# A four-layer graph network on one core: layer 0's results loaded by quarters, row stores on ScalarE, the last half block finished tile by tile

## The chip, the cores and the metric

The kernel runs on one core of a Trainium2 chip. The metric is the device time of one execution in microseconds. A core has TensorE (PE in the profile, with its weight loads as PEld), VectorE (DVE), ScalarE (ACT), GpSimd (POOL) and SyncE (SP), which work side by side and wait for each other by semaphores, and 16 DMA engines that move data between the main memory and the on-chip memory. A DMA is issued by an engine's instruction stream: SP, ACT or POOL. If an instruction there has to wait, those behind it wait too.

## What is computed

Four layers run one after the other over x (16 batches, 1024 nodes, 256 features) with one sparse matrix adj (1024 x 1024). Everything is float32.

```python
# layer 0
S   = sigmoid(relu(h_u @ W1[:d] + h_v @ W1[d:] + b1) @ W2 + b2)      # one score for each pair u, v
a_t = einsum('buv,bud->bvd', S * adj, h)
m_t = einsum('uv,bud->bvd', adj, h) * h
z   = beta1 * h + beta2 * (a_t @ Wa + ba) + beta3 * (m_t @ Wm + bm)
# layer 1
z   = z + relu((adj @ z) @ W.T + b)
# layers 2 and 3 (each)
feats = data @ W1.T
f1    = feats @ W2 + b2
coefs = softmax(leaky_relu(f1[:, :, None] + f1[:, None, :]) + adj, axis=-1)
out   = coefs @ feats + bias2 + data
```

## The kernel before

Because adj is sparse, the scores S are made only for its non-zeros. An earlier part of the program lists them for each node (up to 32 slots, the first 16 of each node and the rest packed into extra rows). There is a second arm of the program (from L1435 on) for a dense adj; it doesn't run here.

The 16 batches are worked in NGR = 4 groups of GB = 4.

*The scores*, `score_steps` (L717), are a generator of small steps: POOL gathers rows of v_d (L708), DVE adds and takes the relu and the weights (L825, L827), ACT sums (L831), and POOL scatters finished scores to a dense table in main memory, `dense_d` (L713). They are not a stage of their own: `Side.along` (L888) lets each step of the main work pay for a fraction of such a step (`PACE`), so that they run beside the matmuls, a group ahead of where they are used.

*The main work of a group.* `score_free` (L942) has earlier made the part of layer 0 that needs no scores and stored it by batch in `zb_d`, features on the partitions, 1024 nodes twice (for the two halves of the features), 1 MB a batch. For each group there follow:

- `with_edges` (L1120), the stage the first part of the change touches. It goes over four blocks of QN = 256 columns (v = 0 to 3), and in each block over eight tiles ut of 128 source nodes. Below, a *unit* is one (v, ut). In a unit, SP loads a piece of the score table, `gd` (512 KB, four buffers, `load_gd`, L904), ACT copies it to `gc` in another order (L1129, two buffers), and PE multiplies: 4 batches x 2 feature halves = 8 products, 16 matmul instructions of 256 columns. At the end of a block DVE adds the eight sums to the block's columns of z (L1152). The batches' z tiles must have been loaded from zb_d by then. In group 0, SP also loads the turned adj (`adj_sb<-adjT_d`, 512 KB each, eight of them) in odd units of the blocks 1 and 2, and ACT takes its exponential (L1118) in the blocks 2 and 3.
- `layer_one` (L1202): `projected` (L1157) makes the rows y, `neighbours` (L1185) multiplies them with pieces `adjT_in` (three buffers) that SP loads at L1191.
- `front` and `sums` (L1004, L1085) for layers 2 and 3. `sums` sums two half blocks of nodes (v = 0, 1), four tiles of 128 nodes each, and ends with `finish`: that of layer 2 is in `second` (L1267), that of layer 3 in `third` (L1297).

*The z loads.* `load_z` (L916) takes four z tiles and appends their loads to the list `z_loads`. For groups 1 to 3, `group_layers` (L1355) of the group before takes three of them from the list near its end (`next_z`, L1367); what remains is done in `with_edges` (L1136): one load of a whole 1 MB tile in every even unit, until the list is empty. For group 0 all four are loaded there, in the units 0, 2, 4 and 6 of block 0. For the later groups only the fourth is, in unit 0.

*What orders the work.* `paced` (L123) makes an instruction wait until PE has finished the product that was recorded some number of products back: 12 for a z load, 24 for a gd load, 16 for an adj_sb load and for a gc copy. The rest of the order on each engine comes from the order of the program, in which the framework may move loads ahead; on SP all loads and stores of this part stand in one stream.

*The last group* treats its batches in two pairs. While the first pair does layer 1, the second pair's rows y are made by `far_ahead` (L1401) and stored to `y_d` (L1404, eight stores of 256 KB). `by_lists` (L1207) gathers such rows with POOL along the lists and sums them on DVE (L1244), for the first six node tiles, with some sums stored to `part_d` by SP (L1248); all of this runs beside PE's work on the first pair.

*Layer 3's end*, `third`'s `finish` (L1318), handles two tiles at a time: two ACT copies out of the sums, one reciprocal on DVE of the two weights' totals, two DVE steps that divide and add the residual (L1328), and one store of 256 KB. Stores are put in the list `later`, and issued by ACT a tick later (L1333, shown in the profile at the caller's lines L998 and L1002).

Of the kernel before, what the change touches and what calls it, by code (L numbers as in the profile page):

```python
# [11 lines left out]
F32 = mybir.dt.float32  # L12
I32 = mybir.dt.int32
U32 = mybir.dt.uint32
AF = mybir.ActivationFunctionType
ALU = mybir.AluOpType
AX = mybir.AxisListType
P = 128

GB = 4  # L20
# [50 lines left out]
def gnn_stack_kernel(  # L71
# [27 lines left out]
    nc = tc.nc  # L99
    B, N, D = x.shape  # L100
# [3 lines left out]
    NV = N // HN  # L104
    HT = HN // P
    QN = HN // 2
# [3 lines left out]
    small = ctx.enter_context(tc.tile_pool(name="small", bufs=4))  # L110
    psum = []

    def bank():
        return psum[-1].tile([P, HN], F32, tag="bank", name="bank")
# [8 lines left out]
    def paced(ins, back=6):  # L123


        if recent:
            after(tc, ins, [recent[max(0, len(recent) - back)]], mybir.DependencyClass.Sync, "keeps pace")
        return ins
# [122 lines left out]
    zb_d = dram.tile([B, P, DH * N], F32, name="zb_d")  # L251
# [41 lines left out]
    def node_pairs(t):  # L293
        return t.rearrange("p (h n) -> p h n", h=DH)
# [80 lines left out]
    with ExitStack() as stack:  # L375
# [15 lines left out]
        for t in range(NT):  # L391
# [10 lines left out]
            out=below, in_=ones, pattern=[[1, P]], compare_op=ALU.is_gt, fill=0.0, base=0, channel_multiplier=-1,  # L402
# [40 lines left out]
        for t in range(NT):  # L443
# [5 lines left out]
            for r in range(SLOTS // 8):  # L449
                s = slice(8 * r, 8 * r + 8)  # L450
                nc.vector.max(out=slot_a[:, t, s], in_=src)
                if r < SLOTS // 8 - 1:
                    nc.vector.match_replace(
                        out=left, in_to_replace=slot_a[:, t, s], in_values=src, imm_value=-1.0
# [12 lines left out]
        ps = bank()  # L467
# [36 lines left out]
        to = prep1.tile([P, NF], F32, name="to")  # L504
# [183 lines left out]
    with tc.If(listed > 0) as arm:  # L688
        with ExitStack() as stack:
# [226 lines left out]
            def load_z(g):  # L916

                z = [node_pairs(wide_z.tile([P, DH * N], F32, tag="wide", name="z")) for _ in range(GB)]

                def load(i):  # L920
                    return nc.sync.dma_start(z[i], node_pairs(zb_d[g * GB + i]))

                z_loads.extend((load, i) for i in range(GB))
                return z

            z_loads = []
# [56 lines left out]
            four = stack.enter_context(tc.tile_pool(name="four", bufs=4, reuse_waits="tile"))  # L983
# [7 lines left out]
            later = []  # L991
# [128 lines left out]
            def with_edges(g, hw, z):  # L1120

                doing[0] = "edges"
                for v in range(N // QN):
                    cols = slice(v * QN, (v + 1) * QN)
                    acc = [[bank() for _ in range(DH)] for _ in range(GB)]
                    for ut in range(NT):
                        gd = first_gd.pop(0) if first_gd else load_gd(g, v, ut, back=BACK)
                        gc = gc_pool.tile([P, GB, QN], F32, tag="gc", name="gc")
                        paced(nc.scalar.activation(gc, gd.rearrange("p n i -> p i n"), AF.Copy), 16)  # L1129
                        for i in range(GB):  # L1130
                            for eh in range(DH):
                                product(
                                    acc[i][eh][:, :QN], hw[i][:, ut, eh * P : (eh + 1) * P], gc[:, i, :],
                                    start=ut == 0, stop=ut == NT - 1,
                                )
                        if z_loads and ut % 2 == 0:  # L1136
                            load, i = z_loads.pop(0)
                            paced(load(i), 12)
                        if (to_load or to_exp) and ut % 2 and v:
                            if v > 1 and to_exp:  # L1140
                                exponential(to_exp.pop(0))
                            if to_load:
                                jt = to_load.pop(0)
                                paced(nc.sync.dma_start(ea[:, jt, :], adjT_d[jt]), 16)
                                to_exp.append(jt)
                        yield 3.4 if g or v else 1
                    if v == N // QN - 1:
                        while to_exp:
                            exponential(to_exp.pop(0))
                    for i in range(GB):  # L1150
                        for eh in range(DH):
                            nc.vector.scalar_tensor_tensor(  # L1152
                                z[i][:, eh, cols], acc[i][eh][:, :QN], zbias[:, eh : eh + 1], z[i][:, eh, cols],
                                ALU.add, ALU.add,
                            )

            def projected(z, keep=None):  # L1157

                doing[0] = "one"
                y = [node_major("y") for _ in range(2)]  # L1160
                for jt in range(0, NT, 2):
                    for i in range(2):
                        ps = bank()
                        for k in range(2):
                            for dh in range(DH):
                                product(
                                    ps[:, k * D : (k + 1) * D], z[i][:, dh, (jt + k) * P : (jt + k + 1) * P],
                                    l1wT[:, dh, :], start=dh == 0, stop=dh == DH - 1,
                                )
                        nc.scalar.activation(  # L1170
                            y[i][:, jt : jt + 2, :], ps.rearrange("p (t d) -> p t d", t=2), AF.Copy
                        )
                        if keep:
                            keep(i, slice(jt, jt + 2), y[i][:, jt : jt + 2, :])
                        yield 1.7
                return y
# [120 lines left out]
            def third(z, i, b):  # L1297
                turned_back = []

                def early(v, jt):  # L1300
                    if v == 0 and jt == 2:
                        for dh in range(DH):
                            nc.scalar.activation(
                                z[i][:, dh, :], z[i][:, dh, :], AF.Identity, bias=gat3.bias2[:, dh : dh + 1]
                            )
                    if jt < NT - 2:
                        return
                    ps = bank()
                    for k in range(2):
                        it = v * HT + (jt - NT + 2) * 2 + k  # L1310
                        for dh in range(DH):
                            nc.tensor.transpose(
                                ps[:, k * D + dh * P : k * D + (dh + 1) * P],
                                z[i][:, dh, it * P : (it + 1) * P], ident,
                            )
                    turned_back.append(ps)

                def finish(v, acc):  # L1318
                    for c in range(0, HT, 2):
                        ps = turned_back.pop(0)  # L1320
                        it = v * HT + c
                        st = four.tile([P, 2, D + 1], F32, tag="st", name="st")
                        share = small.tile([P, 2], F32, tag="share", name="share")
                        for k in range(2):
                            nc.scalar.activation(st[:, k, :], acc[c + k][:, : D + 1], AF.Copy)  # L1325
                        nc.vector.reciprocal(share, st[:, :, D])
                        for k in range(2):
                            nc.vector.scalar_tensor_tensor(  # L1328
                                st[:, k, :D], st[:, k, :D], share[:, k : k + 1], ps[:, k * D : (k + 1) * D],
                                ALU.mult, ALU.add,  # L1330
                            )
                        to = out[b + i, it * P : (it + 2) * P].rearrange("(t p) d -> p t d", p=P)
                        later.append([1, functools.partial(nc.scalar.dma_start, to, st[:, :, :D])])  # L1333
                return finish, early

            def pair_layers(b, z, first):
# [64 lines left out]
            def far_ahead(z, main):  # L1401

                both = y_d.rearrange("(t p) (i d) -> p t i d", p=P, i=2)
                y = yield from projected(z, lambda i, ts, y: nc.sync.dma_start(both[:, ts, i, :], y))  # L1404
                gone, far = 0.0, Side(by_lists(msg))
                rest = neighbours(y, z, slice(FAR * P, N))

                def slots():
                    nonlocal gone
                    for us in itertools.chain(rest, main):  # L1410
                        gone += us
                        yield us * (0.68 if gone < 82 else 0.61)

                far.along(slots(), dict.fromkeys(PACE, 1))
                for _ in far.steps:
                    pass
                yield 0

            msg = []
            for g in range(NGR):  # L1420
                hw, z = loaded.pop(0)
# [141 lines left out]
```

## Time and profile before

| | |
|---|---|
| three runs, median | 3143.56 us (3133.77 to 3150.67) |
| profiled execution | 3123.2 us |
| its span, first to last instruction | 3121.5 us |
| mean granted clock of TensorE | 0.998 |
| PE busy | 3074.8 us (99% of the span) |
| DVE, ACT, POOL busy | 2352.6, 1945.1, 1878.9 us |
| moved by DMA | 700 MB, 224 GB/s on average |
| edge stage of group 0, first to last matmul | 942.07 to 1062.74 us |
| edge stages of groups 1, 2, 3 begin at | 1495.49, 2045.31, 2598.04 us |

In the profile's lists a row has the start in us, the length in us, the engine, the line of the kernel, the operation, what it writes `<-` what it reads, and how many such instructions were merged into the row (x64). A float32 product is two matmul instructions. What stands in square brackets is idle time of that engine just before the row, and whose result ended it. SPq and ACTq are DMA issues by SP and ACT, with the time that the issue took, not the transfer. A table by stretches has for each stretch the busy time of the five engines, the granted clock, the mean busy share of the 16 DMA engines and what they moved in GB/s.

### The profile page before, as it was taken

What the parts mean: (1) busy time and instruction counts of PE and PEld (TensorE: products, weight loads), DVE (VectorE), ACT (ScalarE), POOL (GpSimd) and SP (SyncE); (2) the same over time, 40 slices, a digit from 0 to 9 for tenths busy, and PEclk for the clock granted to TensorE, in tenths of its full rate; (3) what the DMA queues carried; (4) which work ended last, traced back from release to release, by engine and by line L of the source; (5) the groups of instructions that cost most, each with busy time, mean ns of one, the idle gap of its engine ahead of it and who ended that gap; (6) DMA issues with size and microseconds to landing.
All of it is one profiled execution on the core that took longest, in us unless ns stands there. A gap on an engine that the chain in (4) does not pass through costs nothing. (4 is left out here: it accounts for less than half of the span.)

```text
span 3121.5 us, 39024 instructions
## 1 busy us (share of the span) xinstructions
PE 3074.8 (99%) x11954; PEld 2179.2 (70%) x11954; DVE 2352.6 (75%) x3183; ACT 1945.1 (62%) x6520; POOL 1878.9 (60%) x1483
## 2 busy tenths in 40 slices
PE   9999999999999999999999999999999999999999
PEld 5544555545547756888875688888568888858888
DVE  7887777768774678999667899966789982157844
ACT  3345565656667876787887677788667764414242
POOL 1156787777664577777666776766777770076600
PEclk9999999999999999999999999999999999999999
DMA  9998898888889776568877665887765565485500
GB/s 321 331 331 310 270 313 260 273 242 253 254 290 331 229 214 202 156 185 285 285 233 207 209 165 171 266 284 232 219 206 164 159 207 166 132 262 156 164 2 28
DMA packets 288420, 699.96 MB, mean 224 GB/s; under 512 B 46141, under 2 KB 141178, under 8 KB 281034
## 3 DMA queue, kind: packets, MB, share of 16 engines
q0 software_dynamic: 128224, 387.80, 42.5%
q1 hardware_dynamic: 132538, 258.46, 23.7%
q10 hardware_dynamic: 27440, 51.13, 4.3%
q8 instruction: 96, 1.57, 0.2%
q14 instruction: 122, 1.00, 0.1%
HBM read 565.83 MB, written 131.41 MB: 223 GB/s over the span
## 5 line engine op out<-in xcount | busy, mean ns | idle before, releaser
L831 ACT ACTIVATE z<-z 128x256 f32<-128x256 f32 x2432 | 979.0, 406 | 574.1 <-DVE z L827 549.0
L825 DVE TENSOR_TENSOR z<-z,u 128x1024 f32<-128x1024 f32 x608 | 738.9, 1220 | 374.8 <-PE bank L131 262.4
L131 PE MATMUL bank<-feats,m 128*128 128x257 f32 x4096 | 909.0, 380 | 0.7 <-ACT st L1325 0.5
L708 POOL DMA_INDIRECT z<-v_d,slot_v x512 | 662.2, 1293 | 376.0 <-ACT z L831 208.1
L131 PEld LDWEIGHTS bank<-feats,m 128*128 128x128 f32 x4096 | 769.4, 190 | 111.2 <-ACT st L1325 1.3
L713 POOL DMA_INDIRECT dense_d<-gt,slot_at x512 | 674.5, 1317 | 184.4 <-issue 130.3
L827 DVE SCALAR_TENSOR_TENSOR z<-z,w2r 128x1024 f32<-128x1024 f32 x608 | 737.3, 1219 | 9.0
L131 PE MATMUL bank<-gc,hw 128*128 128x256 f32 x2048 | 451.8, 382 | 15.6 <-ACT gc L1129 10.5
L831 ACT ACTIVATION_READ_ACCUMULATOR z<-z 128x1 f32 x2432 | 461.6, 190 | 0.0
L131 PE MATMUL bank<-adj_sb,h 128*128 128x512 f32 x1024 | 442.3, 592 | 3.3 <-ACT st L333 2.0
L131 PEld LDWEIGHTS bank<-gc,hw 128*128 128x128 f32 x2048 | 386.6, 190 | 80.2 <-ACT gc L1129 20.7
L1099 DVE SCALAR_TENSOR_TENSOR m<-rho,tau,adj_sb 128x512 f32<-128x512 f32 x512 | 375.8, 742 | 65.6 <-PE bank L131 62.7
L131 PE MATMUL bank<-adjT_in,y 128*128 128x512 f32 (+1 forms) x960 | 403.4, 581 | 6.0 <-DMA adjT_in<-adjT_d 5.9
L131 PEld LDWEIGHTS bank<-adj_sb,h 128*128 128x128 f32 x1024 | 194.3, 190 | 242.7 <-issue 237.5
L131 PEld LDWEIGHTS bank<-adjT_in,y 128*128 128x128 f32 x960 | 182.0, 191 | 221.0 <-issue 203.8
L131 PE MATMUL bank<-w,hT 128*128 128x512 f32 (+1 forms) x1024 | 334.9, 487 | 0.0
L1129 ACT ACTIVATE gc<-gd 128x1024 f32<-128x1024 f32 x128 | 264.7, 2069 | 88.4 <-PE bank L131 74.9
L131 PEld LDWEIGHTS bank<-w,hT 128*128 128x128 f32 x1024 | 194.8, 191 | 141.5 <-issue 118.4
L131 PE MATMUL bank<-g_wT,z 128*128 128x257 f32 x1024 | 231.4, 380 | 1.6 <-ACT st L1325 1.1
L131 PEld LDWEIGHTS bank<-g_wT,z 128*128 128x128 f32 x1024 | 191.8, 190 | 33.2 <-issue 3.1
L708 POOL DMA_INDIRECT z<-v_d,x_node x96 | 124.2, 1294 | 128.6 <-ACT z L831 96.6
L1152 DVE SCALAR_TENSOR_TENSOR z<-bank,zbias,z 128x256 f32<-128x256 f32 x128 | 54.6, 480 | 111.7 <-PE bank L131 111.4
(168 smaller groups left out, 2379.4 us busy)
## 6 DMA issues: line engine op xcount, KB each, us to landing
gd<-dense_d SPq DMA_DIRECT2D x128, 512.0 KB
dense_d<-zero ACTq DMA_DIRECT2D x64, 512.0 KB
adjT_in<-adjT_d SPq DMA_DIRECT2D x112, 256.0 KB
h<-in_x_dram SPq DMA_DIRECT2D x19, 1024.0 KB
u_d<-st SPq DMA_DIRECT2D x64, 256.0 KB
v_d<-st SPq DMA_DIRECT2D x64, 256.0 KB
hw_d<-st SPq DMA_DIRECT2D x64, 256.0 KB
u<-u_d POOLq DMA_DIRECT2D x32, 512.0 KB
```

Source lines behind the costliest of these rows:

```text
L131: recent.append(nc.tensor.matmul(*args, **kw))
L708: return nc.gpsimd.indirect_dma_start(out=dst, out_offset=None, in_=src[:], in_offset=bass.IndirectOffsetOnAxis(ap=at, axis=0), **how,)
L713: return nc.gpsimd.indirect_dma_start(out=dst[:], out_offset=bass.IndirectOffsetOnAxis(ap=at, axis=0), in_=src, in_offset=None,)
L825: paced(nc.vector.tensor_tensor(z, z, u, ALU.add))
L827: nc.vector.scalar_tensor_tensor(zk, zk, 0.0, w2r[:, None, :].to_broadcast([P, GB, D]), ALU.max, ALU.mult)
L831: nc.scalar.activation(zk[:, c, :], zk[:, c, :], AF.Copy, accum_out=s[:, k, c : c + 1])
L1099: nc.vector.scalar_tensor_tensor(m, r[:, cols], ta[:, kt : kt + 1], ea[:, kt, cols], ALU.max, ALU.mult)
L1129: paced(nc.scalar.activation(gc, gd.rearrange("p n i -> p i n"), AF.Copy), 16)
L1152: nc.vector.scalar_tensor_tensor(z[i][:, eh, cols], acc[i][eh][:, :QN], zbias[:, eh : eh + 1], z[i][:, eh, cols], ALU.add, ALU.add,)
```

## The change

There are three edits.

1. A z load can load one quarter of a tile: the 256 columns of block v, for both feature halves, 256 KB. `with_edges` no longer empties `z_loads` in block 0. It keeps the list over the four blocks and loads, in even units, the quarter of each tile that belongs to the block at hand; the list is cleared after the last block. Group 0 so has sixteen loads of 256 KB, four in each block, in place of four of 1 MB in block 0. Groups 1 to 3 load the quarters of their fourth tile in unit 0 of each block. The three tiles that `next_z` loads are loaded whole as before.
2. The eight stores of `far_ahead` to `y_d` are issued by ACT, not SP.
3. In the last half block of the last batch, `finish` handles one tile at a time: four rounds of one copy, one reciprocal, one dividing step and one store of 128 KB, where there were two rounds of double size; and these four stores are issued by SP, not ACT. All other half blocks stay as they were.

```diff
-                def load(i):
-                    return nc.sync.dma_start(z[i], node_pairs(zb_d[g * GB + i]))
+                def load(i, v=None):
+                    cols = slice(None) if v is None else slice(v * QN, (v + 1) * QN)
+                    return nc.sync.dma_start(z[i][:, :, cols], node_pairs(zb_d[g * GB + i])[:, :, cols])
...
-                        if z_loads and ut % 2 == 0:
-                            load, i = z_loads.pop(0)
-                            paced(load(i), 12)
+                        if ut % 2 == 0 and ut // 2 < len(z_loads):
+                            load, i = z_loads[ut // 2]
+                            paced(load(i, v), 12)
...
                     if v == N // QN - 1:
+                        z_loads.clear()
                         while to_exp:
...
                 def finish(v, acc):
+                    last = b + i == B - 1 and v == NV - 1
                     for c in range(0, HT, 2):
                         ps = turned_back.pop(0)
                         it = v * HT + c
-                        st = four.tile([P, 2, D + 1], F32, tag="st", name="st")
-                        share = small.tile([P, 2], F32, tag="share", name="share")
-                        for k in range(2):
-                            nc.scalar.activation(st[:, k, :], acc[c + k][:, : D + 1], AF.Copy)
-                        nc.vector.reciprocal(share, st[:, :, D])
-                        for k in range(2):
-                            nc.vector.scalar_tensor_tensor(
-                                st[:, k, :D], st[:, k, :D], share[:, k : k + 1], ps[:, k * D : (k + 1) * D],
-                                ALU.mult, ALU.add,
-                            )
-                        to = out[b + i, it * P : (it + 2) * P].rearrange("(t p) d -> p t d", p=P)
-                        later.append([1, functools.partial(nc.scalar.dma_start, to, st[:, :, :D])])
+
+                        for ks in ((0,), (1,)) if last else ((0, 1),):
+                            n, k0 = len(ks), ks[0]
+                            st = four.tile([P, 2, D + 1], F32, tag="st", name="st")[:, :n, :]
+                            share = small.tile([P, 2], F32, tag="share", name="share")[:, :n]
+                            for k in ks:
+                                nc.scalar.activation(st[:, k - k0, :], acc[c + k][:, : D + 1], AF.Copy)
+                            nc.vector.reciprocal(share, st[:, :, D])
+                            for k in ks:
+                                nc.vector.scalar_tensor_tensor(
+                                    st[:, k - k0, :D], st[:, k - k0, :D], share[:, k - k0 : k - k0 + 1],
+                                    ps[:, k * D : (k + 1) * D], ALU.mult, ALU.add,
+                                )
+                            to = out[b + i, (it + k0) * P : (it + k0 + n) * P].rearrange("(t p) d -> p t d", p=P)
+                            queue = nc.sync if last else nc.scalar
+                            later.append([1, functools.partial(queue.dma_start, to, st[:, :, :D])])
...
-                y = yield from projected(z, lambda i, ts, y: nc.sync.dma_start(both[:, ts, i, :], y))
+                y = yield from projected(z, lambda i, ts, y: nc.scalar.dma_start(both[:, ts, i, :], y))
```

## Prediction

> **What bounds the kernel now.** I read the page's busy times first, then the busy times by stretch with the DMA share, then the PE timeline of the stage that adds layer 0's edge part, then what SP and ACT did there, and last the row stage and the tail.
>
> ```profile
> PE 3074.8 (99%) x11954; PEld 2179.2 (70%) x11954; DVE 2352.6 (75%) x3183; ACT 1945.1 (62%) x6520; POOL 1878.9 (60%) x1483
> ```
>
> TensorE is busy 99% of 3121.5 us, so only what removes a hole in PE's stream (46.7 us in all) or shortens the tail can help. A group's edge stage has four blocks of columns (v = 0 to 3), each of 128 matmul instructions of 256 columns. At group 3, where nothing disturbs it, 512 of them take 2598.04 to 2708.55, 110.5 us, or 0.216 each. At group 0 they take 942.07 to 1062.74, 120.7 us: about 10 us of holes. By blocks v = 0 to 3 of group 0 (columns: us, then busy of PE, PEld, DVE, ACT, POOL, then clock, DMA share, GB/s):
>
> ```profile
> 942.07:973.65 31.58, 27.97 (x129) 23.98 (x128) 8.31 (x14) 19.34 (x32) 11.71 (x11) 1.00 0.99 362
> 973.65:1002.60 28.95, 28.16 (x129) 23.82 (x128) 16.05 (x19) 24.78 (x49) 15.64 (x13) 1.00 0.91 316
> 1002.60:1033.36 30.76, 28.92 (x132) 24.13 (x130) 21.24 (x27) 29.76 (x62) 13.60 (x12) 1.00 0.91 321
> 1033.36:1062.74 29.38, 28.53 (x128) 24.09 (x129) 17.67 (x21) 29.38 (x67) 11.14 (x9) 1.00 0.72 225
> ```
>
> Against 27.6 us (a quarter of 110.5) the blocks lose 4.0, 1.3, 3.2 and 1.8 us. Block 0 loses with the DMA engines full (0.99, 362 GB/s) and ACT idle a third of the time; blocks 2 and 3 lose with ACT busy 97% and 100%. These are two different limits. Block 0 on PE, then SP, then ACT:
>
> ```profile
> 942.07 13.98 PE L131 MATMUL bank<-gc,hw 128*128 128x256 f32 x64
> 958.23 3.72 PE L131 MATMUL bank<-gc,hw 128*128 128x256 f32 x16 [2.18 <-ACT gc L1129]
> 963.38 28.22 PE L131 MATMUL bank<-gc,hw 128*128 128x256 f32 x128 [1.44 <-ACT gc L1129]
> 992.33 17.86 PE L131 MATMUL bank<-gc,hw 128*128 128x256 f32 x80 [0.73 <-ACT gc L1129]
> ```
>
> ```profile
> 946.15 0.32 SPq L907 DMA_DIRECT2D gd<-dense_d  x1
> 947.88 0.32 SPq L921 DMA_DIRECT2D z<-zb_d  x1
> 949.61 0.32 SPq L907 DMA_DIRECT2D gd<-dense_d  x1
> ```
>
> ```profile
> 956.16 2.02 ACT L1129 ACTIVATE gc<-gd 128x1024 f32<-128x1024 f32 x1 [3.27 <-PE bank L131]
> 961.31 3.96 ACT L1129 ACTIVATE gc<-gd 128x1024 f32<-128x1024 f32 x2 [3.13 <-DMA gd<-dense_d]
> ```
>
> PE waits for gc, ACT for gd. The fifth gd was issued at 946.15 and used at 956.16, the sixth at 949.61 and 961.31: 10.0 and 11.7 us for 512 KB, with 1 MB of z issued between them. The wait credited to PE at 956.16 had ended by then on PE's side (PE was out of work from about 956.0), so I read it as the same late gd. At 992.33 one more hole of some 1.6 us follows a gd that was 8.4 us on its way.
>
> The rows of the last group (waits of PE from 2708 to 2813) and the tail:
>
> ```profile
> PE bank L131 <- DMA adjT_in<-adjT_d: 4.7, 3, 3.3
> ```
>
> ```profile
> 3113.82 1.69 ACT L1325 ACTIVATE st<-bank 128x257 f32<-128x257 f32 x4 [13.07 <-PE bank L131]
> 3114.67 0.17 DVE L1326 RECIPROCAL share<-st 128x2 f32<-128x2 f32 x1 [6.17 <-ACT st L1325]
> ...
> 3115.89 1.42 ACTq L1002 DMA_DIRECT2D out_dram<-st  x2
> 3115.97 0.87 DVE L1328 SCALAR_TENSOR_TENSOR st<-st,share,bank 128x256 f32<-128x256 f32 x2
> ```
>
> [...] a gd issued behind 1 MB of z on the same queue took 11.7 us, others in the stage 6.5 to 8.4. [...]
>
> **The change, part by part.** In the built program the compute instructions of PE, ACT and POOL stand in the same order as before; SP's queue changes, ACT gains eight stores and loses two, and DVE's order differs only in the last half block.
>
> 1a. *Group 0's z in quarters.* Sixteen loads of 256 KB, four in each block, for four of 1 MB in block 0. Block 0 sheds 3.15 MB: it moved 362 x 31.58 = 11.4 MB and would move 8.3 MB, 300 GB/s in 27.6 us. The fifth and sixth gd then have 0.79 and up to 1.57 MB less ahead of them, 2.2 and 4.3 us at 362 GB/s, against holes of 2.4 and 1.7 us. Gain at most 4.0; I take 3.6.
>
> 1b. *What the three other blocks pay.* Each takes 1.05 MB more. Block 1: 9.15 + 1.05 MB in 28.95 us is 352 GB/s, block 2: 9.87 + 1.05 in 30.76 is 355, block 3: 6.6 + 1.05 in 29.38 is 261. At block 0's rate of 362 for a share of 0.99 the first two come to 0.96 and 0.97: nearly full. On SP each quarter stands ahead of an adj_sb load and two gd. Its wait on PE (12 products back) ends about 2 us before that of the adj_sb load behind it (16 back, but one unit later), so it blocks nothing by its wait; what it costs is its bytes: 0.26 MB at 362 GB/s, 0.72 us later for the gd behind it. There are eight such gd in blocks 1 and 2. Bounds: 0 (spare share takes it) to 8 x 0.72 = 5.8. [...] In block 2 ACT is the limit, so most of it is hidden there; without that cover it would cost the 2.9 us. I take 1.0 in block 1 and 0.3 in block 2, 0 in block 3 (DMA share 0.72, ACT full).
>
> 1c. *Groups 1 to 3.* Only the fourth z of each group comes in this stage; 1 MB at the start becomes 256 KB in each block. Group 1 has a hole of 0.94 us at 1520.19 after a gd late by 1.96 us on ACT: I take 0.8 (0 to 1.3). Group 2's holes at its start (1.5 and 2.8 us) wait for DVE's finishing step L1328, not for a load: 0 (0 to 0.5). Group 3 has no holes: 0. The 21 more issues of 0.32 us on SP lie in SP's waits on PE (345 us at L907).
>
> 2. *Row stores on ScalarE.* Removed from SP: 8 x 0.36 us and its waits for the copies. ACT gets them between copies of 0.60 us that have 1.13 us of idle before each, so 0.36 us fits; if it did not, PE's next banks would wait. Does SP send anything sooner? Three adjT_in pieces are loaded long before; the fourth needs the first one's buffer, which PE has read at 2722.36 + 8 x 0.214 = 2724.1, and it was issued at 2724.28. So 0.2 at most. The gathers wait for all eight stores; the last was issued on SP at 2723.2, right at the end of its copy, and the first gather began at 2726.07. The queue doesn't change that. PE's 4.7 us stay: SP's adjT_in loads stand behind stores of list sums that wait 25.3 us for DVE, and those are not touched. I take 0.1 (0.5 gained to 1.7 lost, one copy's period, should the last store land later).
>
> 3. *Tail.* The first reciprocal can start after one copy, 3114.24 for 3114.67, but DVE then has two reciprocals more (0.16 plus 0.09 to the next step): 4 x 0.44 + 4 x 0.16 + waits again end near 3116.8. The last store is 128 KB for 256 KB. [...] Before, it took 3116.93 to the span's end at 3121.5. I take 0.5 (0.3 lost to 1.2 gained).
>
> Sum: 3.6 - 1.3 + 0.8 + 0.1 + 0.5 = 3.7 us gained. The profiled execution (3121.5 span, 1.7 around it, 3123.2) would be 3119.5. The runs' median stands 20 us above it, so I take the difference over: 3143.56 - 3.7 = 3139.9.
>
> **Rivals.**
> A, the forecast, 3139.9, own range 3136 to 3143: chance 0.58.
> B, the queue is filled later instead (slower): in blocks 1 and 2 of group 0 the eight gd behind a quarter come too late. The gains sum to 5.0 us, so it decides from 0.63 us of PE stall for each of the eight, and 0.72 of pure transfer is there[...]. With latency growing near a full queue to 1 us each: 8.0 - 5.0 = 3.0 lost, 3146.6. For it: shares of 0.96, and one gd of block 1 is late already. Against: ACT is the later one in block 2, and a slower PE gives loads more time. Chance 0.14.
> C, all of it pays: block 0's 4.0, block 1's 1.3 (less backlog carried over), group 1's 1.3, group 2's 0.5, 3.0 of the row holes and 1.2 of the tail: 11.3, 3132.3. For it: the share of 0.99. Against: the row holes have another cause. Chance 0.14.
> D, it does nothing: in block 0 ACT's copies, kept two ahead at most, or PE's own pacing end the wait, and the quarters cost what is left: 3143.0. Against: ACT idles 12 us of the 31.6 there. Chance 0.14.
>
> **Range and chances.** The three runs of before spread over 16.9 us (0.54%), and the profiled one lay below them all; 0.5% (15.7 us) is about what a measurement of this kernel can tell from no change. None of the cases passes 0.5% by itself; only scatter does, or a part of case C that the profile hides. From C's 3132 less 8 of scatter to B's 3146.6 plus 5: 3124 to 3152. Faster by over 0.5% 0.14 (half of C, a tenth of A and some of D), slower 0.04 (a quarter of B), within 0.82.
>
> **What would show it.** Right: block 0 of group 0 near 28 us at a DMA share near 0.85, the holes ahead of its fifth and sixth unit gone; blocks 1 and 2 at shares of 0.95 or more and not over 1 us longer; first gather still some 3 us after the last row store; the three adjT_in holes still there; span's end about 4 us after the last DVE step. Wrong: ACT waiting for gd in blocks 1 and 2 by more than 5 us in all (B), row holes gone (C), or block 0 still over 30 us (D).

## The result and the profile after

The changed kernel takes 3140.05 us in the median of 14 runs (3133.81 to 3153.14), the kernel before 3140.80 in 14 runs beside it (3131.79 to 3150.67). The ratio is 1.0003, with a 95% interval from 0.9990 to 1.0016: no difference that can be measured. The time forecast, 3139.9, is met, but that is luck in part: the gain behind it, 3.7 us or a ratio of 0.9988, lies just outside the interval, and the number is met because 14 runs put the kernel before 2.8 us below the three that the forecast started from. So the question is where those few microseconds went.

The profiled execution of the changed kernel took 3138.14 us with a span of 3136.4; that of the kernel before had 3121.5. These 15 us are no effect of the change: 7 of them are there when group 0's edge stage begins (949.28 for 942.07), before any changed line has run, and 7 more in group 1's edge stage, which comes back below. So stages are compared here, not spans.

Group 0's edge stage, blocks 0 to 3, in the kernel after. The cuts are at the first product of each block; columns as in the prediction:

```profile
949.28:979.56 30.28, 28.39 (x129) 24.07 (x128) 10.24 (x17) 20.22 (x36) 13.42 (x13) 1.00 0.87 300
979.56:1009.50 29.94, 28.14 (x129) 23.88 (x127) 16.28 (x19) 24.96 (x49) 15.47 (x13) 1.00 0.97 328
1009.50:1040.05 30.55, 28.52 (x130) 23.92 (x129) 20.80 (x26) 29.25 (x61) 14.17 (x12) 1.00 0.98 352
1040.05:1070.25 30.20, 28.67 (x129) 24.09 (x130) 17.73 (x22) 29.46 (x67) 11.16 (x9) 1.00 0.82 263
```

The DMA shares came close to what the prediction worked out (0.87 in block 0 for 0.85, 0.97 and 0.98 in blocks 1 and 2 for 0.96 and 0.97). Block 0 is shorter, the others together longer, and the sum is 120.97 us for 120.67 before. On PE:

```profile
949.28 14.24 PE L131 MATMUL bank<-gc,hw 128*128 128x256 f32 x64
965.11 3.72 PE L131 MATMUL bank<-gc,hw 128*128 128x256 f32 x16 [1.59 <-ACT gc L1130]
969.10 27.89 PE L131 MATMUL bank<-gc,hw 128*128 128x256 f32 x128 [0.27 <-ACT gc L1130]
998.79 17.89 PE L131 MATMUL bank<-gc,hw 128*128 128x256 f32 x80 [1.80 <-ACT gc L1130]
```

The hole ahead of the fifth unit fell from 2.18 to 1.59 us, the one ahead of the sixth from 1.44 to 0.27; the hole in block 1 (ahead of 998.79) grew from 0.73 to 1.80. ACT's wait for gd in blocks 1 and 2 is 5.6 us, for 5.5 before. (The prediction's table cut the blocks up to 0.4 us off; cut like this one, those of before are 31.77, 29.16, 30.35 and 29.38.)

The last group's rows. First what SP did between the first pair's layer 1 and its adjT_in pieces, then the waits of PE:

```profile
2764.36 10.61 SPq L1250 DMA_DIRECT2D part_d<-msg  x3
2775.08 0.37 SPq L1193 DMA_DIRECT2D adjT_in<-adjT_d  x1
```

```profile
PE bank L131 <- DMA adjT_in<-adjT_d: 3.8, 1, 3.8
PE bank L131 <- issue: 1.3, 1, 1.3
```

The 5 us of holes are still there (3.8 + 1.3, for 4.7 in three holes before), behind three stores of list sums. ACT issued the last row store at 2737.87, and the first gather began at 2741.00, 3.1 us later (2.9 before). The tail, on DVE:

```profile
3129.54 0.16 DVE L1332 RECIPROCAL share<-st 128x1 f32<-128x1 f32 x1 [5.74 <-ACT st L1331]
...
3131.02 0.87 DVE L1334 SCALAR_TENSOR_TENSOR st<-st,share,bank 128x256 f32<-128x256 f32 x2
```

DVE ends at 3131.89, 2.77 us after the last copies began at 3129.12 (before: 3.02), and the span ends 4.5 us after that (4.7). From the copies' start to the end it is 7.3 us for 7.7: 0.4 gained. The traces of the experiments below agree: this stretch took 7.7 to 9.5 us in the four executions with the old tail, and 7.1 to 7.6 in nine of the ten with the new one (8.6 in the tenth).

### The profile page after: what moved, and what is told of

The parts are those of the page before. It is cut to its first block, busy times and chain, and to the rows that moved or that the text cites. A ratio compares the mean times of both kernels' runs of the same rounds, so it can differ in the third digit from the quotient of the medians.

```text
span 3136.4 us, 39102 instructions
## 1 busy us (share of the span) xinstructions
PE 3078.7 (98%) x11954; PEld 2181.5 (70%) x11954; DVE 2352.4 (75%) x3185; ACT 1946.6 (62%) x6520; POOL 1888.1 (60%) x1483
## 3 DMA queue, kind: packets, MB, share of 16 engines
q8 instruction: 96, 1.57, 0.2%
## 5 line engine op out<-in xcount | busy, mean ns | idle before, releaser
L708 POOL DMA_INDIRECT z<-v_d,slot_v x512 | 669.2, 1307 | 390.6 <-ACT z L831 215.6
L713 POOL DMA_INDIRECT dense_d<-gt,x_at x96 | 120.4, 1255 | 29.2 <-issue 26.5
```

The lines of the kernel that those rows point to most:

```text
L708: return nc.gpsimd.indirect_dma_start(out=dst, out_offset=None, in_=src[:], in_offset=bass.IndirectOffsetOnAxis(ap=at, axis=0), **how,)
L713: return nc.gpsimd.indirect_dma_start(out=dst[:], out_offset=bass.IndirectOffsetOnAxis(ap=at, axis=0), in_=src, in_offset=None,)
```

## The experiments

Theory to test: quarters only move a wait that is set by bytes. Rivals: the profile after was unlucky and a gain is there; or the stage is set by something else, ScalarE's copies or the order in SP's queue. Three sets of four kernels ran, each with the kernel before beside it: experiments 1 to 4 (kernel before 3137.2 us, 75 runs), 5, 6, 7 and 9 (3136.88, 43 runs), and 8 and 10 to 12 (3127.64, 39 runs). Ratios are to the kernel before of the same set, with the 95% interval in brackets; stages and blocks are read from one profiled execution of each kernel. Line numbers differ by a few between kernels.

**1. The first edit alone** (`z_only`). The quarters as after; row stores and `finish` as before:

```diff
-  y = yield from projected(z, lambda i, ts, y: nc.scalar.dma_start(both[:, ts, i, :], y))
+  y = yield from projected(z, lambda i, ts, y: nc.sync.dma_start(both[:, ts, i, :], y))
```

> Edit 1 alone. Theory 1 (what block 0 of group 0 gains, the later blocks give back): the edge stage of group 0 takes 120 to 122 us as in the changed kernel (120.97), with block 0 near 30 and blocks 1 to 3 near 29.7, 31 and 30.2; the whole time equals that before within 2 us. Theory 2 (the profiled execution of the changed kernel was an unlucky one, and edit 1 does gain its 2 to 4 us): the stage takes 116 to 118 us here, and the time is 2 to 4 us below that before.

Measured: 3141.13 us, 1.0011 (1.0000 to 1.0023). No gain; if anything a loss. The forecast for this edit alone (2.3 us in group 0 and 0.8 in group 1, a ratio of 0.9990) is outside the interval. Group 0's stage took 128.17 us, 3.4 of it for half clock; the 124.8 that remain are still above the 120 to 122 expected, with the excess in blocks 2 and 3 (33.3 and 31.0).

**2. The other two edits alone** (`rows_tail`): z whole, by SP, as before; rows and tail as after. Against the kernel before:

```diff
-  y = yield from projected(z, lambda i, ts, y: nc.sync.dma_start(both[:, ts, i, :], y))
+  y = yield from projected(z, lambda i, ts, y: nc.scalar.dma_start(both[:, ts, i, :], y))
...
+ for ks in ((0,), (1,)) if last else ((0, 1),):
```

> Edits 2 and 3 alone, z loaded whole as before. A second execution of the old edge stage of group 0: theory 1 expects 120 to 121 us with 31.5 in block 0; theory 2 expects 120 to 121 as well, so that the two kernels of this call differ by 0 (theory 1) or by 3 to 4 us (theory 2) in this stage. The holes before the adjT_in pieces of the last group stay at 4 to 6 us under both. Whole time: 0 to 1 us below before.

Measured: 3136.39 us, 0.9998 (0.9984 to 1.0013). Nothing to be seen, and 0.6 us could not be. Group 0's stage took 123.49 us, 121.8 without its half-clock loss; the holes in the last group's rows were there (4.5 us in five).

**3. No z loads in the edge stages** (`z_none`). DVE writes zeros in place of the quarters:

```diff
 def load(i, v=None):
     cols = slice(None) if v is None else slice(v * QN, (v + 1) * QN)
+    if v is not None:
+        return nc.vector.memset(z[i][:, :, cols], 0.0)
     return nc.sync.dma_start(z[i][:, :, cols], node_pairs(zb_d[g * GB + i])[:, :, cols])
```

> The changed kernel with the quarter loads left out: DVE fills those quarters of z with zero, so layer 0's part without edges is missing there. 4 MB less in group 0's edge stage, nothing else changed. Theory 1 (bytes): block 0 near 28, block 1 near 28, together 3 to 4 us less than in the changed kernel, stage 115 to 117. Rival (ScalarE sets the stage, whatever is loaded): blocks 2 and 3 stay at 30 to 31 and block 0 and 1 too lose at most 1 us in all, stage 120.

Measured: 3129.93 us, 0.9974 (0.9960 to 0.9988), so that this kernel is some 8 us (4 to 13) below the kernel before. Little of that lies in group 0's stage: it took 119.76 us, where the rival had put it (120), and not the 115 to 117 of the theory. Where the rest lies isn't shown. Blocks 0 and 1 of group 0:

```profile
945.80:974.87 29.07, 28.05 (x130) 24.16 (x129) 10.13 (x19) 19.53 (x32) 12.34 (x12) 1.00 0.78 252
974.87:1005.27 30.40, 28.15 (x129) 23.88 (x127) 17.64 (x23) 24.99 (x49) 15.98 (x13) 1.00 0.87 288
```

```profile
994.55 18.28 PE L131 MATMUL bank<-gc,hw 128*128 128x256 f32 x80 [2.25 <-ACT gc L1132]
```

Block 0 without z is 2.9 us shorter than with whole z (31.8 and 32.2). But block 1, also without z, is longer than before, with the hole of the kernel after in the same place, and longer (2.25 us for 1.80): the gd behind it was issued at 982.81 and landed 9.6 us later, with no z load under way. So in this execution the hole is there without the quarters.

**4. Twice the bytes** (`z_double`): behind each of group 0's quarters SP copies the same 256 KB within main memory.

```diff
     paced(load(i, v), 12)
+    if g == 0:
+        paced(nc.sync.dma_start(again_d[v * GB + i], node_pairs(zb_d[i])[:, :, cols]), 12)
```

> The changed kernel with each of group 0's sixteen quarter loads followed on SP's queue by a copy of the same 256 KB from main memory to main memory (a result nobody reads). Theory 1 (bytes): the same price again, 0.7 us for each of the eight gd behind it in blocks 1 and 2 and some in block 0, stage 124 to 128 us. Rival (ScalarE sets the stage): 121 to 122 us.

Measured: 3144.92 us, 1.0023 (1.0011 to 1.0036), by the ratios 6 us above the changed kernel; group 0's stage took 126.84 us, 125.1 without its half-clock loss. Its blocks are then 30.5, 30.4, 32.2 and 32.1 us, for 30.3, 29.9, 30.5 and 30.2 in the changed kernel. Added bytes do cost, against the rival, and they cost most in the last two blocks.

**5. Quarters in group 0 only** (`z_g0`). By then, all three kernels with quarters had a longer block 0 in group 1.

```diff
-if ut % 2 == 0 and ut // 2 < len(z_loads):
+if g == 0 and ut % 2 == 0 and ut // 2 < len(z_loads):
     load, i = z_loads[ut // 2]
     paced(load(i, v), 12)
+if g and z_loads and ut % 2 == 0:
+    load, i = z_loads.pop(0)
+    paced(load(i), 12)
```

> The changed kernel, but with quarters in group 0 only; the fourth z of groups 1 and 2 is loaded whole at the first unit, as before. In the traces so far the three kernels with quarters start group 1's edge stage 3 us slower (block 0 of group 1, less the time that TensorE ran at half clock: 34.7, 35.4 and 35.4 us, against 31.8, 31.9 and 31.5 in the three without). Theory (quarters cause it): block 0 of group 1 is back at 31.5 to 32 us, group 0 stays as in the changed kernel (block 0 near 30.2, blocks 1 and 3 each some 0.8 longer than with whole z), and the time is about 3 us below the changed kernel's, 3137 against 3140. Rival (chance of single executions): group 1's block 0 is again near 35 or anywhere between, and the time is the changed kernel's, 3140.

Measured: 3136.20 us, 1.0002 (0.9989 to 1.0015), and group 1's block 0, less its half-clock time, was 34.6 us with a whole z. My theory that the quarters cause it falls: it is scatter of single executions.

**6. The z loads in another queue** (`z_whole_act`): the kernel before, with the whole z loads of the edge stage issued by ACT.

```diff
-def load(i):
-    return nc.sync.dma_start(z[i], node_pairs(zb_d[g * GB + i]))
+def load(i, queue=nc.sync):
+    return queue.dma_start(z[i], node_pairs(zb_d[g * GB + i]))
...
-    paced(load(i), 12)
+    paced(load(i, nc.scalar), 12)
```

> The kernel before, with the whole z loads of the edge stage issued on ScalarE's queue and not on SP's; same bytes at the same places of the program. Theory of bytes (the loads of block 0 are limited by what the DMA engines move): block 0 of group 0 stays at 31.5 to 32.5 us, time as before, 3137 to 3141. Theory of order (gd is late because 1 MB stands ahead of it in the same queue, as the prediction's sum of 0.79 and 1.57 MB took it): with z in another queue the gd of the fifth and sixth unit arrive 2 us or more sooner, and block 0 falls to 29.5 us or less with no quarter at all.

Measured: 3146.14 us, 1.0031 (1.0020 to 1.0042): slower by some 10 us, where no change was expected; where these lie was not followed up. Block 0:

```profile
947.63:980.38 32.75, 28.43 (x130) 24.07 (x128) 9.27 (x16) 19.32 (x32) 12.67 (x12) 1.00 0.99 361
```

```profile
963.50 2.02 ACT L1129 ACTIVATE gc<-gd 128x1024 f32<-128x1024 f32 x1 [4.78 <-DMA gd<-dense_d]
```

It moved 11.8 MB (11.4 in the prediction's block 0) at a share of 0.99, and was no faster. The gd for which ACT waits 4.78 us was issued by SP at 951.71, with no z ahead of it in SP's queue (ACT issued z at 945.25 and 953.44), and still was 11.7 us on its way. So its place in SP's queue is not what makes it late; of the two theories, the one of bytes remains.

**7. Two gc copies in eight on VectorE** (`gc_split`), in blocks 2 and 3 of groups 0 to 2:

```diff
-paced(nc.scalar.activation(gc, gd.rearrange("p n i -> p i n"), AF.Copy), 16)
+if g < NGR - 1 and v > 1 and ut % 4 == 3:
+    paced(nc.vector.tensor_copy(gc, gd.rearrange("p n i -> p i n")), 16)
+else:
+    paced(nc.scalar.activation(gc, gd.rearrange("p n i -> p i n"), AF.Copy), 16)
```

> The changed kernel, with the fourth and eighth gc copy of blocks 2 and 3 of the edge stage moved from ScalarE to VectorE in groups 0 to 2 (12 copies). Theory (ScalarE, 97% and 98% busy there, sets these blocks in group 0): ScalarE's share falls to about 85%, blocks 2 and 3 of group 0 together fall from 60.7 us or more to about 57 to 58, and the time falls by 3 us. Rival (gd late behind the quarters, or VectorE's own steps, set them): the blocks stay within 1 us of 60.7 and the time is unchanged or, should the copies hold up VectorE's side work, 2 us longer.

Measured: 3134.14 us, 0.9993 (0.9982 to 1.0005). Blocks 2 and 3 of group 0:

```profile
1000.84:1031.02 30.18, 28.54 (x130) 24.15 (x129) 22.31 (x27) 26.41 (x63) 13.77 (x12) 1.00 0.97 348
1031.02:1058.65 27.63, 27.63 (x130) 24.32 (x129) 19.89 (x24) 25.47 (x63) 9.31 (x9) 1.00 0.86 288
```

Block 3 runs without a hole, at the 27.63 us of group 3's blocks: ScalarE set it. Block 2 hardly moves. Of its holes of 0.7 and 0.8 us on PE, the first follows a gd for which ACT waited 2.3 us, and ahead of the second ACT worked without a break: both limits are there.

**8. The same edit on the kernel before** (`gc_before`): the diff of 7 alone, nothing of the change.

> The kernel before (whole z loads, rows stored by SP, old tail), with the fourth and eighth gc copy of blocks 2 and 3 moved from ScalarE to VectorE in groups 0 to 2. Theory (block 3 of group 0 is set by ScalarE's load, with whole z as with quarters): block 3 falls from 29.4 to 27.6 us as it did with quarters, block 0 stays near 32, the stage takes 119 to 120 us, 2 to 3 us less than with whole z so far (120.7 to 123.8); time 3134 to 3136 against 3137 of before. Rival (only the quarters make room for it): block 3 stays at 29.4.

Measured: 3124.13 us, 0.9987 (0.9980 to 0.9994): a small gain that can be measured. Blocks of group 0: 31.87, 29.17, 29.83 and 27.62; block 3 is free with whole z too.

**9. The loads that SP holds up, issued by ACT** (`adj_act`). My edit missed its aim: it moved the adjT_in loads of layer 1 in all groups, not in the last alone.

```diff
-nc.sync.dma_start(a, adjT_d[jt][:, cols])
+(nc.scalar if n == HN and jt > 2 else nc.sync).dma_start(a, adjT_d[jt][:, cols])
```

> The changed kernel, with the adjT_in loads of the last group's full-width half blocks issued by ScalarE from the fourth tile on (its queue is empty there), so that they no longer stand behind the stores of list sums on SP. Theory (they stand behind those stores, which wait for DVE): the two holes of TensorE ahead of adjT_in products, 3.8 and 1.3 us, go, and with them the stretch of 3.4 us at half clock that follows the first, 1.7 us: 5 to 7 us gained, 3134 against 3140, ratio to the kernel before near 0.998. Rival (the loads are late by their bytes or their buffers, or the hole only moves to the next piece): holes of 4 us or more stay in this stage and the time is within 1 us of the changed kernel's.

Measured: 3156.60 us, 1.0048 (1.0026 to 1.0070), slower. In groups 0 to 2 ACT does side work for the scores, and the loads now stand in its stream: from the end of group 1's edge stage to the start of group 2's it took 441.96 us, where the 13 other executions have 433.2 to 435.4. The waits of PE there, for 2.2 us in three holes, none over 1.0, in the kernel after:

```profile
PE bank L131 <- DMA adjT_in<-adjT_d: 6.7, 2, 5.7
```

In the last group the same ten loads were with ACT, too, and yet the holes did not go:

```profile
2793.54 27.73 PE L131 MATMUL bank<-adjT_in,y 128*128 128x512 f32 x64 [1.59 <-DMA adjT_in<-adjT_d]
2825.53 5.49 PE L131 MATMUL bank<-adjT_in,y 128*128 128x512 f32 x6 [4.26 <-DMA adjT_in<-adjT_d]
```

ACT issued the first of them only at 2790.51, between row copies that ran late: they waited for PE up to 4.4 us, for 1.1 to 1.3 us in experiment 10, and the trace doesn't show why.

**10. The same in the last group alone** (`adj_last`):

```diff
-nc.sync.dma_start(a, adjT_d[jt][:, cols])
+(nc.scalar if at_end and n == HN and jt > 2 else nc.sync).dma_start(a, adjT_d[jt][:, cols])
...
+at_end.append(1)
 for _ in far_ahead(z[2:], pair_layers(g * GB, z[:2], layer_one(z[:2]))):
```

> The changed kernel, with the adjT_in loads of the full-width half blocks issued by ScalarE from the fourth tile on, in the last group's far-ahead stage only. (The kernel adj_act was meant to do this, but moved those loads in all groups, into a ScalarE queue full of side work; its 15 us say nothing of this stage.) Theory (these loads wait behind stores of list sums on SP): the holes of 3.8 and 1.3 us ahead of adjT_in products shrink to under 1 us in all, and no half-clock stretch of 3.4 us follows them: 5 to 7 us gained, from 3137 to 3140 down to 3131 to 3134. Rival (something else holds the stage, TensorE's own late results or the loads' landing): holes of 3 us or more stay and the time is within 2 us of the changed kernel's.

Measured: 3119.81 us, 0.9971 (0.9961 to 0.9982). PE's products with adjT_in, and ACT's issues:

```profile
2744.99 55.10 PE L131 MATMUL bank<-adjT_in,y 128*128 128x512 f32 x128
```

```profile
2748.62 14.06 ACTq L1194 DMA_DIRECT2D adjT_in<-adjT_d  x5
```

All 128 are one row without a hole; the kernel after had 3.8 and 1.3 us of holes in it. (A hole of 1.0 us ahead of an earlier product, whose load stayed with SP, is still there.) From the end of group 3's edge stage to the end of the program it took 408.06 us for 413.20 after and 412.95 before: 5.1 us. The interval in time, 5.6 to 12.2 us, begins a little above that. But 413 is at the low end: eleven executions, experiment 9 among them, took 412.7 to 416.1 us here, and the three with this edit (10, 11 and 12) 406.1 to 408.1.

**11. Both** (`gc_adj`): the diffs of 7 and 10 together, on the changed kernel.

> The changed kernel with both edits, the gc copies of gc_split and the loads of adj_last. Theory: the two add, since they lie in different stages: 3 us of group 0's edge stage and 5 to 7 us of the last group's rows, 3128 to 3132, ratio to the kernel before 0.997 to 0.9985. Rival (holes move rather than go): within 2 us of gc_split alone, 0.9993.

Measured: 3111.66 us, 0.9953 (0.9936 to 0.9969), some 15 us below the kernel before, which the changed kernel equals within 0.16%: faster than both, and better than the 0.997 to 0.9985 expected. The two edits apart (0.9993 and 0.9971) would give 0.9964, which the interval holds. Group 0's stage took 116.48 us, the last stretch 406.34.

**12. More copies on VectorE** (`gc_half`): as 11, and every second gc copy of blocks 0 and 1 of group 0:

```diff
-if g < NGR - 1 and v > 1 and ut % 4 == 3:
+if g < NGR - 1 and v > 1 and ut % 4 == 3 or g == 0 and v < 2 and ut % 2:
```

> gc_adj, and in group 0 every second gc copy of blocks 0 and 1 on VectorE too, where a copy takes 1.12 us for ScalarE's 2.08 and VectorE is busy a third of the time. Theory of bytes (what is left of the holes in blocks 0 and 1 is gd landing late at a DMA share of 0.9 to 0.97): a copy that is 1 us shorter moves gd's buffer free sooner, but the loads are no faster; blocks 0 and 1 stay within 1 us of 29.6 and 29.8. Rival (the chain of gd, copy and product sets these blocks): both fall by 1 us or more, towards 28.5.

Measured: 3118.37 us, 0.9970 (0.9960 to 0.9980). Blocks 0 and 1, less 1.7 us for half clock in block 0: 29.8 and 30.3 us, no shorter, as the theory of bytes expected. The faster copy (1.12 us on VectorE for 2.08 on ScalarE, both in experiment 7) did not help here. The version to keep is 11.

## Why the prediction was right about the time and wrong about the gain

Block lengths of group 0, from the starts of the products, less half of the time that PE worked at half clock (see the last section), in us. "Measured" is the mean with quarters less that with whole z:

| block | whole z (before, 2) | quarters (after, 1, 5, 9, 10), mean and range | no z (3) | forecast | measured |
|---|---|---|---|---|---|
| 0 | 31.8, 32.2 | 29.8 (29.2 to 30.3) | 29.1 | -3.6 | -2.1 |
| 1 | 29.2, 29.3 | 30.2 (29.8 to 31.2) | 30.4 | +1.0 | +1.0 |
| 2 | 30.4, 30.9 | 31.2 (30.2 to 33.3) | 30.9 | +0.3 | +0.6 |
| 3 | 29.4, 29.4 | 30.1 (29.4 to 31.0) | 29.4 | 0 | +0.7 |
| sum | 121.2 | 121.3 | 119.8 | -2.3 | 0.1 |

The five executions with quarters sum to 118.9 to 124.8 us, so the 0.1 is known to a microsecond or so at best (without experiment 1 it is -0.7). Of the 2.4 us between forecast and measured, 1.5 lie in block 0, 0.7 in block 3 and 0.3 in block 2.

*Step 1a, block 0.* Right in its direction and cause (bytes in block 0), too large. The prediction let quarters take away nearly all of the two holes. But experiment 3 shows that with no z at all block 0 still loses 1.4 us against 27.63, so 2.9 was the most there was, and the quarters got 2.1 of it. The sum "0.79 and up to 1.57 MB less ahead of them" treated the delay as a place in SP's queue; experiment 6 shows that it isn't. So the 11.7 us of a gd behind z, which the prediction reckoned as a place in that queue, don't show such an order. The trace of before had a sign of it, block 0's DMA share of 0.99: with ACT as the issuer of z (experiment 6) it was 0.99 again, and the block took 32.75 us, for 31.8 and 32.2 with SP. What the last 1.4 us are is open.

*Step 1b, the other blocks.* The size taken for block 1 is right, 1.0 us, by luck, for the reason is wrong. It counted 0.72 us for each 256 KB ahead of a gd; the same hole is there, at 2.25 us, with no z load. It stands behind a gd that is 9.1 to 9.6 us on its way, issued right behind an adj_sb load. With block 0 over sooner PE only reaches it sooner, as I read it. (The hole that the prediction puts at "some 1.6 us" in the kernel before is 0.73 us in its own line.) What makes this gd slow at a share of 0.87 is open. Block 3, "0 in block 3 (DMA share 0.72, ACT full)", is the term that was put at nothing without a good reason: it took 0.7 us more. In the four executions without a quarter load (before, 2, 3 and 6) it took 29.35 to 29.38 us, in the five with quarters 29.4 to 31.0, and with twice the bytes (4) 32.1. ACT full was no cover: it did not make up what a late gd cost there. In the kernel after, the second gd of block 3, issued behind an adj_sb load and a quarter, was 8.7 us on its way (before: 6.4), and ACT, which has no time to lose there, stood still for it:

```profile
1042.32 2.09 ACT L1130 ACTIVATE gc<-gd 128x1024 f32<-128x1024 f32 x1 [0.74 <-DMA gd<-dense_d]
```

With two copies less on ACT (experiments 7 and 11) block 3 has no hole even with quarters: the loss needs both. Whether the quarters keep a part of their gain there can't be told: the stage took 117.3, 116.5 and 118.7 us with quarters (7, 11 and 12, without half clock) and 118.5 with whole z (8), and in time nothing of it shows (0.9993 for 7, 0.9987 for 8).

*Step 1c, groups 1 to 3.* Group 3 as said, no hole. The 0.8 us in group 1 can't be told: its block 0, less half-clock time, varies from 30.8 to 35.4 us over the 14 executions, and group 2's from 30.9 to 37.6, with whole z and with quarters.

*Step 2, rows on ScalarE.* Right: first gather 3.1 us after the last row store, holes unchanged. Experiments 10 to 12 show the reason: the holes of 3.8 and 1.3 us are gone once the adjT_in loads no longer stand behind stores that wait for DVE. Experiment 9 shows the limit: behind late copies on ACT they are back, with 1.6 and 4.3 us. Another issuing engine brought no gain for the row stores (experiment 2, with the tail: 0.9998) and none for z (experiment 6: 1.0031). But the same move was worth about 0.3% for adjT_in, because what it saved was not the 0.4 us of an issue but a wait of other instructions in the same stream: in the kernel after the load issued at 2775.08 stands behind three stores with 0.32 us of issue each that took SP 10.61 us; the last could begin only at 2774.65, right behind DVE's sum, which ended at 2774.62. Moved in all groups (experiment 9) it cost 15 us, with the loads in the stream of ACT's side work.

*Step 3, the tail.* 0.4 us in the profile for a forecast of 0.5; in the time it can't be seen. What the smaller last store gives, no run here takes by itself.

The total: forecast 2.3 in group 0, 0.8 in group 1, 0.1 and 0.5. Measured 0.0, not to be told, 0.0 and 0.4. Rival D, "it does nothing", named the right end for group 0, and its sign is there: block 0 is still over 30 us. Of its reasons, ACT's copies as the limit in block 0 have experiment 12 against them; PE's own pacing was not tested. Rival B's mechanism, eight late gd, isn't seen: ACT's wait for gd in blocks 1 and 2 stayed at 5.6 us. The sign set for B, over 5 us, could not tell, for it was 5.5 before the change. Rival C is out, since the row holes had the cause that was read.

## What to carry to other kernels

Before moving bytes to a later block, ask what that block waits for: here block 0 gained 2.1 us, the three blocks behind it gave back about as much (1.0, 0.6 and 0.7), and ACT, before busy all through block 3, hid nothing of its 0.7. Read a queue for what its instructions wait for, not for what they cost: here eight row stores moved for nothing, and ten loads moved out from behind stores that wait for VectorE were worth about 0.3%. The same change in all groups, with ACT's queue busy in three of them, cost half a per cent, so I would move such loads only where the other queue is empty.

## What the runs showed of the hardware

*Half the clock after a hole.* In the row stage of the kernel after, stretches of 3.41 us side by side (busy PE second, clock third from the end):

```profile
2772.91:2776.33 3.42, 2.63 (x7) 0.84 (x5) 2.13 (x4) 0.00 (x0) 2.50 (x4) 1.00 0.79 210
2776.33:2779.74 3.41, 0.40 (x1) 0.30 (x2) 1.29 (x2) 0.00 (x0) 2.80 (x3) 1.00 0.91 334
2779.74:2783.15 3.41, 3.41 (x5) 1.35 (x4) 1.99 (x3) 0.00 (x0) 2.48 (x4) 0.50 0.88 262
2783.15:2786.57 3.42, 2.13 (x6) 0.71 (x5) 0.75 (x1) 0.00 (x0) 2.55 (x3) 1.00 0.98 341
```

PE was busy for 0.40 us of the second stretch, and the third is at half clock (0.50) though PE is busy all through it. At group 1's start the same (mean ns of a product after the count): at half clock and, below it, just after.

```profile
L131 PE MATMUL bank<-gc,hw 128*128 128x256 f32 x14 | 6.3, 644 | 6.4 <-ACT gc L1130 6.4
```

```profile
L131 PE MATMUL bank<-gc,hw 128*128 128x256 f32 x76 | 16.6, 379 | 0.0
```

In the traces of before and after the half clock lasts 3.41, 6.83 or 10.24 us at a time, leaving out the end of the program, and begins a whole number of 3.413 us after the one before; so I laid a grid of such stretches over each trace and counted. Over 14 executions, without their first 25 us and from 3050 us on, all 48 full-clock stretches on that grid with PE busy for less than 0.43 of the stretch were followed by one at half clock, and none of the 391 between 0.45 and 0.90 was; of the ten in between three were. From this count I estimate that a hole of about 1.9 us (0.57 of 3.41) costs up to 1.7 us more (half of 3.41) if it lies within one stretch, and nothing more if the grid cuts it into halves. Leaving out the end of the program, before had three stretches at half clock, after seven, and `adj_last` one: with its hole went the half-clock stretch behind it, which is why 5.1 us of holes is not all that it could gain.

*Where executions differ.* The stretch between the edge stages of groups 0 and 1 took 432.5 to 432.9 us in 12 of the 14 executions, group 3's edge stage 110.51 in all; the starts of the edge stages of groups 1 and 2 vary by 5 and 7 us beyond the clock. In seven of them PE has a hole of 5.0 to 6.5 us within group 1's first four units, in the other seven one of 1.1 to 2.9, among them all four of the last set, beside which the kernel before was 9 us faster, too. In the kernel after, the copy that ends this hole begins at 1515.41, though all products that it can wait for are recorded as done by 1511.04, and its gd had landed long before. No wait in the trace explains it, and it stays open.
